# A four-layer graph network on one core: half products for the last weight, norm constants on GpSimd, and a new issue order for the main loop

## The chip, the cores and the metric

The kernel runs on one core of a Trainium2 chip. The metric is device time in microseconds (us) of one execution; the inputs are in device memory before it starts. All runs told here were fast, at a mean granted TensorE clock of 0.98 in the profiled ones, so they may be compared as they stand. Two kernels are called the same if they differ by less than 2%. A ratio is the mean time of one kernel's fast runs over that of the other's of the same rounds, so it is not quite the ratio of the medians quoted beside it; its 95% interval follows in brackets.

Engines in the profile: PE is TensorE, PEld its weight loads, DVE VectorE, ACT ScalarE, POOL GpSimd, SP SyncE. L348 is line 348 of the profiled kernel; numbers shift between kernels, because lines were added. A timeline row reads: start in us, duration in us, engine, line, operation, output<-inputs, shapes, count, and in brackets how long the engine had been idle just before and what released it.

## The reference, cut to what matters

`x` is 128 batches of 128 nodes by 256 features, in fp32. Four layers, each with a layer norm ahead and a residual behind:

```python
h = max(layernorm(x), 0);  x = x + gated_messages(h, adj)        # layer 0: three gates, two adjacency products
h = max(layernorm(x), 0);  x = x + causal_attention(h)           # layer 1: scores + adj, softmax, value, Wo
h = max(layernorm(x), 0);  x = x + A2(relu(A2(relu(A2 h W1)) W2)) W3   # layer 2: 256 -> 512 -> 1024 -> 256
h = max(layernorm(x), 0);  agg = A_hat h                         # layer 3
x = x + batchnorm(relu(batchnorm(agg W1' + b1)) W2' + b2)        # statistics over all 128*128 rows
```

(This is a condensed form of it.) Only the two batch norms of layer 3 need all batches at once. They cut the kernel into three stages: a long loop, the second product of layer 3 (512 features to 256), and the last batch norm with the residual.

## The kernel before

Batches are worked in 32 groups of four. Every layer is a Python generator that yields after each piece of work. A string, `TURN`, says from which generator the next piece is taken, and one pass through the string is one turn of the main loop. It interleaves the layers of four groups (`g - 1` to `g + 2`) and so steers the order of the instructions in every engine's queue; within a piece the queues can still mix.

```python
    TURN = "CCBCABBCDABCBBCABDDCBADCDDBDCDCBACBBCACACCCbBCBBCBCBBCBCBCBd"
    # ...
        stream = {
            "A": part(layer0, g + 2), "B": bs, "C": layer2(g), "D": ds,
            "b": part(layer1, g + 2), "d": layer3(g),
        }
        for k in TURN:
            next(stream[k], None)
```

The layer norm, four times per group. `inv_sqrt` is an add of eps on VectorE and a power of -0.5 on GpSimd:

```python
        rs = small.tile([P, G], FP, tag="rs", name=f"rs{layer}_{g}")
        inv_sqrt(rs, mv[:, :, 1], LN_EPS)
        sh = small.tile([P, G], FP, tag="sh", name=f"sh{layer}_{g}")
        nc.vector.scalar_tensor_tensor(sh, mv[:, :, 0], -1.0, rs, ALU.mult, ALU.mult)
        h = w.tile([P, G, D], FP, tag="h", name=f"h{layer}_{g}", bufs=3)
        for b in range(G):
            nc.scalar.activation(
                h[:, b, :], xt[:, b, :], AF.Relu, bias=sh[:, b : b + 1], scale=rs[:, b : b + 1]
            )
```

Most weight products of the loop are already done in seven half-size products instead of eight (Strassen's scheme in Winograd's form). That needs four sums of the activations' quarters:

```python
        engine.tensor_tensor(s1, a21, a22, ALU.add)
        engine.tensor_tensor(s2, s1, a11, ALU.subtract)
        engine.tensor_tensor(s4, a12, s2, ALU.subtract)
        engine.tensor_tensor(s3, a11, a21, ALU.subtract)
```

The second product of layer 3 is a plain one, after a per-column batch norm and ReLU on ScalarE:

```python
        for i in range(DC):
            po = bank([P, T], f"po_{g}_{i}")
            for j in range(FC):
                nc.tensor.matmul(
                    po, bw2T[:, j, i * P : (i + 1) * P], z[j],
                    start=(j == 0), stop=(j == FC - 1),
                )
            nc.vector.tensor_scalar(O[g][:, i, :], po, b2_c[:, i : i + 1], None, ALU.add)
            nc.vector.bn_stats(stats2[:, i, g, :], O[g][:, i, :])
```

## Time and profile before

The median was 2703.4 us. The stages of the profiled execution (2701.6 us):

| stage | us | limit |
|---|---|---|
| start to the first product of the second stage, with the loop's 32 turns | 2400.2 | TensorE |
| second product of layer 3 | 222.5 | TensorE |
| last batch norm, residual, output | 78.8 | transfers |

### The profile page before, as it was taken

The page shows a single profiled execution, that of the slowest core. Times are in us where ns is not written, and L with a number is a line of the kernel's source. Part 1 is how long each engine was busy: PE and PEld are TensorE (multiplying, and loading weights), DVE is VectorE, ACT ScalarE, POOL GpSimd, SP SyncE. Part 2 cuts the span into 40 slices and gives each one's busy share as a digit, 9 for nine tenths or more (in the row PEclk, how much of TensorE's full clock was granted, in tenths as well). Part 3 has the DMA queues.
Part 4 walks back from the last instruction along what each step waited for, and adds up shares of the span by engine and source line. Part 5 has one row for each costly group of instructions (what it writes and reads, how often), then busy time and mean ns, then how long its engine had stood idle before and what let it go on. Part 6 is the DMA issues. An engine that isn't in the chain of part 4 may idle for free.

```text
span 2701.6 us, 39124 instructions
## 1 busy us (share of the span) xinstructions
PE 2579.3 (95%) x14831; PEld 2216.3 (82%) x14831; DVE 1877.5 (69%) x4612; ACT 1236.5 (46%) x2447; POOL 477.2 (18%) x484
## 2 busy tenths in 40 slices
PE   3899999999999999999999999999999999979994
PEld 3788888889898898888888889889888888944443
DVE  7677777677777877777777777777777775444445
ACT  3444444444444444444444444454444443334435
POOL 3121111121111112111111111111211111110001
PEclk7999999999999999999999999999999999989998
DMA  3000000000000000000000000000000000044449
GB/s 128 8 32 17 32 32 32 32 25 31 27 30 32 32 32 32 32 32 25 24 32 32 32 32 24 32 25 32 32 32 32 32 24 24 24 148 156 156 170 367
DMA packets 61758, 142.17 MB, mean 53 GB/s; under 512 B 4594, under 2 KB 39940, under 8 KB 57604
## 3 DMA queue, kind: packets, MB, share of 16 engines
q1 hardware_dynamic: 51492, 105.21, 10.9%
q0 software_dynamic: 9216, 33.56, 3.2%
q8 instruction: 117, 1.92, 0.3%
q10 hardware_dynamic: 864, 0.92, 0.1%
q14 instruction: 69, 0.57, 0.1%
HBM read 73.08 MB, written 66.58 MB: 52 GB/s over the span
## 4 chain that ended last, share of the span: by engine, by line
PE 62%; DVE 21%; ACT 6%; issue 5%; POOL 4%; DMA 2%; ACTq 0%; DVEq 0%; POOLq 0%; SPq 0%
PE p_x L365 9%; PE po L750 8%; PE p_x L348 6%; PE pu_x L348 4%; PE p_z L365 4%; PE pz_x L365 4%; POOL rs L188 4%; DVE st L285 4%; ACT h L294 3%; DVE uT L307 3%; PE p_z L348 2%; PE pg L304 2%; PE p_y L365 2%; PE pz_z L365 2%; PE pu_z L348 2%
## 5 line engine op out<-in xcount | busy, mean ns | idle before, releaser
L294 ACT ACTIVATE h<-x,sh,rs 128x256 f32<-128x256 f32 x512 | 268.8, 592 | 144.2 <-DVE sh L291 144.2
L188 POOL TENSOR_TENSOR rs<-rs,nhalf 128x4 f32<-128x4 f32 x128 | 130.1, 1017 | 807.6 <-DVE rs L186 807.6
L365 PE MATMUL p_x<-uT,w 128*128 128x256 f32 x1024 | 242.2, 379 | 0.0
L380 ACT COPY p_t<-p_x 128x512 f32<-128x512 f32 (+1 forms) x192 | 98.3, 512 | 298.9 <-PE p_x L365 285.9
L595 ACT ACTIVATE h2T<-h2T 128x512 f32<-128x512 f32 x192 | 120.4, 627 | 232.7 <-DVE h2T L594 232.7
L750 PE MATMUL po<-zi,bw2T 128*128 128x512 f32 x496 | 213.0, 592 | 0.0
L365 PEld LDWEIGHTS p_x<-uT,w 128*128 128x128 f32 x1024 | 189.7, 190 | 23.1
L417 DVE SCALAR_TENSOR_TENSOR gs<-h,gw 128x256 f32<-128x256 f32 x384 | 198.8, 518 | 13.5 <-ACT h L294 1.3
L285 DVE BATCH_NORM_STATS2 st<-x 128x6 f32<-128x256 f32 x512 | 190.7, 414 | 3.4 <-DMA x<-in_x_dram 2.2
L750 PEld LDWEIGHTS po<-zi,bw2T 128*128 128x128 f32 x496 | 94.2, 190 | 118.6 <-issue 107.6
L743 ACT ACTIVATE zi<-zi,sh_bn,sc_bn 128x512 f32<-128x512 f32 x124 | 90.5, 802 | 117.3 <-DMA zi<-z 117.3
L625 POOL DMA_DIRECT2D x<-x x32 | 19.8, 620 | 691.5 <-DVE x L622 691.5
L754 DVE TENSOR_SCALAR o<-po,vecs 128x512 f32<-128x512 f32 x64 | 48.1, 752 | 129.1 <-PE po L750 129.1
L304 PEld LDWEIGHTS pmu<-a2T,u 128*128 128x128 f32 x1024 | 119.5, 192 | 17.1 <-issue 7.4
L348 PEld LDWEIGHTS p_x<-w,h2T 128*128 128x128 f32 x1024 | 124.3, 192 | 3.3
L365 PE MATMUL p_x<-us,w_s 128*128 128x256 f32 x512 | 126.2, 380 | 0.0
L348 PE MATMUL p_x<-w,h2T 128*128 128x128 f32 x1024 | 124.6, 275 | 0.0
L365 PE MATMUL p_x<-uT,w_s 128*128 128x256 f32 x512 | 124.3, 385 | 0.3 <-DVE h2T L594 0.3
L304 PE MATMUL pmu<-a2T,u 128*128 128x128 f32 x1024 | 119.8, 275 | 1.8 <-ACT u L561 1.8
L365 PE MATMUL p_y<-uT,w 128*128 128x256 f32 x512 | 121.1, 379 | 0.0
L365 PE MATMUL p_z<-us,w 128*128 128x256 f32 x512 | 121.0, 379 | 0.0
L365 PE MATMUL p_z<-us,w_s 128*128 128x256 f32 x512 | 121.0, 379 | 0.0
(252 smaller groups left out, 6005.0 us busy)
## 6 DMA issues: line engine op xcount, KB each, us to landing
z<-zo SPq DMA_DIRECT2D x62, 512.0 KB, 2.6
zi<-z SPq DMA_DIRECT2D x31, 1024.0 KB, 4.7
x<-in_x_dram SPq DMA_DIRECT2D x32, 512.0 KB, 3.9
x<-x POOLq DMA_DIRECT2D x32, 512.0 KB, 3.0
x3i<-x POOLq DMA_DIRECT2D x32, 512.0 KB, 6.7
out_dram<-x3i SPq DMA_DIRECT2D x64, 256.0 KB, 6.4
w<-in_L_gnn_W_dram SPq DMA_DIRECT2D x1, 2048.0 KB
w<-in_L_gnn_W_dram SPq DMA_DIRECT2D x1, 1024.0 KB
```

Source lines behind the costliest of these rows:

```text
L188: nc.gpsimd.tensor_tensor(dst, src, nhalf[:, : dst.shape[1]], ALU.pow)
L285: nc.vector.bn_stats(st[:, b, :], xt[:, b, :])
L294: nc.scalar.activation(h[:, b, :], xt[:, b, :], AF.Relu, bias=sh[:, b : b + 1], scale=rs[:, b : b + 1])
L304: nc.tensor.matmul(pm[:, b, :], src[:, b, c * P : (c + 1) * P], aT, start=True, stop=True)
L307: nc.vector.tensor_copy(dst[:, c, :], pm.rearrange("p b n -> p (b n)"))
L348: nc.tensor.matmul(pb[:, rr, :], a_r[r][:, c, rr * P : (rr + 1) * P], b_r[r][:, c, :wide], start=(first and rr == 0 and c == 0), stop=(c = ...
L365: nc.tensor.matmul(pb[:, jj, :], b_r[r][:, c, at : at + P], a_r[r][:, c, :], start=(first and jj == 0 and c == 0), stop=(c == nk - 1), ski ...
L380: nc.scalar.copy(t, pb)
L417: nc.vector.scalar_tensor_tensor(gs, h[:, b, :], 1.0, gw[:, i, :], ALU.mult, ALU.mult, accum_out=gl[:, b, i : i + 1],)
L595: nc.scalar.activation(dst, dst, AF.Relu)
L743: nc.scalar.activation(z[j], z[j], AF.Relu, bias=sh1[:, j : j + 1], scale=sc1[:, j : j + 1],)
L750: nc.tensor.matmul(po, bw2T[:, j, i * P : (i + 1) * P], z[j], start=(j == 0), stop=(j == FC - 1),)
```

## The change

It has four parts. Layer 3's second product becomes seven half products, and the next group's activations and sums are prepared while this group's products run. The layer norms' constants are worked out by GpSimd alone; in exchange its large sums go to VectorE. Two evictions of mT go to ScalarE, and one of hT's two to VectorE. `TURN` is new. The intent is to give TensorE an eighth less work in the second product, and to free VectorE from waiting for GpSimd in the loop.

```diff
-        inv_sqrt(rs, mv[:, :, 1], LN_EPS)
+        nc.gpsimd.tensor_scalar(rs, mv[:, :, 1], LN_EPS, None, ALU.add)
+        nc.gpsimd.tensor_tensor(rs, rs, nhalf[:, :G], ALU.pow)
         sh = small.tile([P, G], FP, tag="sh", name=f"sh{layer}_{g}")
-        nc.vector.scalar_tensor_tensor(sh, mv[:, :, 0], -1.0, rs, ALU.mult, ALU.mult)
+        nc.gpsimd.tensor_scalar(sh, mv[:, :, 0], -1.0, None, ALU.mult)
+        nc.gpsimd.tensor_tensor(sh, sh, rs, ALU.mult)
 # ... layer 1: hT
-            nc.scalar.copy(hT[:, c, :], pt.rearrange("p b n -> p (b n)"))
+            evict = nc.vector.tensor_copy if c else nc.scalar.copy
+            evict(hT[:, c, :], pt.rearrange("p b n -> p (b n)"))
 # ... layer 2: mT, and the sums of h2T's first half
-        mixed(mT, h, a2T, f"pm2_{g}")
+        mixed(mT, h, a2T, f"pm2_{g}", nc.scalar.copy)
-                        nc.vector if q else nc.gpsimd,
+                        nc.vector,
 # ... layer 3: the sums of gT
-        gs = sums(nc.gpsimd, quarters_t(gT), ex)
+        gs = sums(nc.vector, quarters_t(gT), ex)
 # ... the turn
-    TURN = "CCBCABBCDABCBBCABDDCBADCDDBDCDCBACBBCACACCCbBCBBCBCBBCBCBCBd"
+    TURN = "CCCBCCABBDABBCABBDDCBADCDDBDCCDBACBCCABCCACbBCBBCBCBBCBCBCdB"
 # ... second product (core)
-    EARLY = 6
+    EARLY, LATE = 4, 11
+    bw2s = keep.tile([P, 3, FC // 2, D // 2], FP, name="bw2s_late")
+    nc.scalar.dma_start(bw2s, BW2S)
+    BW2R = set_of(bw2T, bw2s)
+    def second(g):
+        # ... four activations, one yield after each
+        nc.vector.tensor_tensor(s1, a21, a22, ALU.add)
+        nc.vector.tensor_tensor(a21, a11, a21, ALU.subtract)
+        nc.vector.tensor_tensor(s2, s1, a11, ALU.subtract)
+        yield
+        def product(r, pb, first):
+            for c in range(FC // 2):
+                nc.tensor.matmul(
+                    pb, BW2R[r][:, c, :], a_r[r][:, c, :],
+                    start=(first and c == 0), stop=(c == FC // 2 - 1), skip_group_check=True,
+                )
+            if r == 1:
+                nc.vector.tensor_tensor(a12, a12, s2, ALU.subtract)
+        # ... eviction by copy or add, then the statistics
+        yield from seven(product, put, [P, T // 2], f"po_{g}", zw)
```

The diff leaves out the sums of the second weights, which GpSimd makes at the start, the way they go through device memory, and the new numbers of buffers for late blocks of x.

More of the change, by code (lines that the diff above doesn't have):

```diff
@@ L188, in inv_sqrt, with quarters, set_of, seven_of @@
         nc.gpsimd.tensor_tensor(dst, src, nhalf[:, : dst.shape[1]], ALU.pow)
+    def quarters(a):
+        k, t = a.shape[1] // 2, a.shape[2] // 2
+        return a[:, :k, :t], a[:, k:, :t], a[:, :k, t:], a[:, k:, t:]
+    def set_of(b, extra):
+        b11, b21, b12, b22 = quarters(b)
+        return b11, b21, b22, extra[:, 2], extra[:, 0], extra[:, 1], b12
+    def seven_of(b, name, extra=None):
+        b11, b21, b12, b22 = quarters(b)
+        if extra is None:
+            extra = weights.tile([P, 3, b.shape[1] // 2, b.shape[2] // 2], FP, name=f"{name}_s")
+        operands = set_of(b, extra)
+        t4n, t1, t2 = operands[3:6]
+        nc.gpsimd.tensor_tensor(t1, b12, b11, ALU.subtract)
+        nc.gpsimd.tensor_tensor(t2, b22, t1, ALU.subtract)
+        nc.gpsimd.tensor_tensor(t4n, b21, t2, ALU.subtract)
+        nc.gpsimd.tensor_tensor(b12, b22, b12, ALU.subtract)
+        return operands
     BW2T = scratch.tile([P, FC, D], FP, name="BW2T")
+    BW2S = scratch.tile([P, 3, FC // 2, D // 2], FP, name="BW2S")
+    bw2s = bw1[:, :3, :].rearrange("p a (b c) -> p a b c", b=FC // 2)
     def turned(dst, src, nr, name):
@@ L246, in prepare @@
         turned(bw2t, bw2, DC, "bw2T")
+        seven_of(bw2t, "bw2t", bw2s)
+        nc.sync.dma_start(BW2S, bw2s)
         nc.sync.dma_start(BW2T, bw2t)
@@ L297, in norm, with mixed @@
         return h
-    def mixed(dst, src, aT, name):
+    def mixed(dst, src, aT, name, evict):
         for c in range(src.shape[-1] // P):
@@ L306, in mixed @@
                 )
-            nc.vector.tensor_copy(dst[:, c, :], pm.rearrange("p b n -> p (b n)"))
-    def quarters(a):
-        k, t = a.shape[1] // 2, a.shape[2] // 2
-        return a[:, :k, :t], a[:, k:, :t], a[:, :k, t:], a[:, k:, t:]
-    def seven_of(b, name):
-        b11, b21, b12, b22 = quarters(b)
-        extra = weights.tile([P, 3, b.shape[1] // 2, b.shape[2] // 2], FP, name=f"{name}_s")
-        t1, t2, t4n = (extra[:, i] for i in range(3))
-        nc.gpsimd.tensor_tensor(t1, b12, b11, ALU.subtract)
-        nc.gpsimd.tensor_tensor(t2, b22, t1, ALU.subtract)
-        nc.gpsimd.tensor_tensor(t4n, b21, t2, ALU.subtract)
-        nc.gpsimd.tensor_tensor(b12, b22, b12, ALU.subtract)
-        return b11, b21, b22, t4n, t1, t2, b12
+            evict(dst[:, c, :], pm.rearrange("p b n -> p (b n)"))
     def sums(engine, a, extra, s3=None):
@@ L371, in columns_by_half, with seven @@
         return product
-    def seven(product, put, shape, name):
+    def seven(product, put, shape, name, pool=None):
         def kept(pb, i):
-            t = w.tile(shape, FP, tag="kept", name=f"{name}_t{i}", bufs=6)
+            t = (pool or w).tile(shape, FP, tag="kept", name=f"{name}_t{i}", bufs=6)
             nc.scalar.copy(t, pb)
@@ L566, in layer1 @@
         uT = w.tile([P, HC1, T], FP, tag="uT", name=f"uT_{g}", bufs=1)
-        mixed(uT, u, a2T, f"pmu_{g}")
+        mixed(uT, u, a2T, f"pmu_{g}", nc.vector.tensor_copy)
         ex = w.tile([P, 3, HC1 // 2, T // 2], FP, tag="us", name=f"us_{g}", bufs=1)
@@ L599, in wide @@
             )
-        s = w.tile([P, G, D], FP, tag="qv", name=f"s_{g}", bufs=1)
+        S = []
         def put_s(ij, pb, other):
             i, j = ij
-            dst = s[:, 2 * i : 2 * i + 2, j * P : (j + 1) * P]
+            if not S:
+                S.append(w.tile([P, G, D], FP, tag="qv", name=f"s_{g}", bufs=1))
+            dst = S[0][:, 2 * i : 2 * i + 2, j * P : (j + 1) * P]
             if other is None:
@@ L620, in layer2 @@
             pr = bank([P, 2, D], f"pr_{g}_{q}")
-            nc.tensor.matmul(pr, a2T, s[:, 2 * q : 2 * q + 2, :], start=True, stop=True)
+            nc.tensor.matmul(pr, a2T, S[0][:, 2 * q : 2 * q + 2, :], start=True, stop=True)
             nc.vector.tensor_tensor(
@@ L632, in layer3 @@
         gT = w.tile([P, DC, T], FP, tag="dT", name=f"gT_{g}", bufs=2)
-        mixed(gT, h, ahT, f"pg_{g}")
+        mixed(gT, h, ahT, f"pg_{g}", nc.vector.tensor_copy)
         ex = w.tile([P, 3, 1, T // 2], FP, tag="ex", name=f"gs_{g}", bufs=2)
-        gs = sums(nc.gpsimd, quarters_t(gT), ex)
+        gs = sums(nc.vector, quarters_t(gT), ex)
         yield
@@ L720 @@
     )
+    zw = zs.enter_context(tc.tile_pool(name="zw", bufs=2, side="right", reuse_waits="tile"))
     bw2T = keep.tile([P, FC, D], FP, name="bw2T")
     nc.scalar.dma_start(bw2T, BW2T)
+    bw2s = keep.tile([P, 3, FC // 2, D // 2], FP, name="bw2s_late")
+    nc.scalar.dma_start(bw2s, BW2S)
+    BW2R = set_of(bw2T, bw2s)
     ORDER = [LAST, *range(LAST)]
@@ L729, in load_z @@
         nc.sync.dma_start(z, Z[ORDER[n]])
-        ZT[ORDER[n]] = [z[:, j, :] for j in range(FC)]
+        ZT[ORDER[n]] = [z[:, :FC // 2, :], z[:, FC // 2 :, :]]
     def load_x3(g, pool, tag):
@@ L734, in load_x3, with put @@
         nc.gpsimd.dma_start(R[g], X3[g])
+    def second(g):
+        zl, zr = ZT[g]
+        ex = zw.tile([P, 2, FC // 2, T // 2], FP, tag="zs", name=f"zs_{g}")
+        a11, a21, a12, a22 = (z[:, :, i * T // 2 : (i + 1) * T // 2] for z in (zl, zr) for i in range(2))
+        s1, s2 = ex[:, 0], ex[:, 1]
+        a_r = a11, a12, a12, a22, s1, s2, a21
+        for j in range(FC):
+            z = ZT[g][j // 2][:, j % 2, :]
+            nc.scalar.activation(
+                z, z, AF.Relu, bias=sh1[:, j : j + 1], scale=sc1[:, j : j + 1],
+            )
[3 more added lines that the diff above has]
+        nc.vector.tensor_tensor(s2, s1, a11, ALU.subtract)
+        yield
+        def product(r, pb, first):
[3 more added lines that the diff above has]
+                    start=(first and c == 0), stop=(c == FC // 2 - 1), skip_group_check=True,
+                )
+            if r == 1:
+                nc.vector.tensor_tensor(a12, a12, s2, ALU.subtract)
+        done = []
+        def put(ij, pb, other):
+            i, j = ij
+            dst = O[g][:, j, i * T // 2 : (i + 1) * T // 2]
+            if other is None:
+                nc.scalar.copy(dst, pb)
+            else:
+                nc.vector.tensor_tensor(dst, pb, other, ALU.add)
+            done.append(j)
+            if done.count(j) == 2:
+                nc.vector.bn_stats(stats2[:, j, g, :], O[g][:, j, :])
+        yield from seven(product, put, [P, T // 2], f"po_{g}", zw)
     for n in range(1, 1 + AT_ONCE):
@@ L738 @@
     sc1, sh1 = bn_affine(stats1, FC, g1_c, be1_c, "bn1", b1_c)
-    ZT[LAST] = [z[:, jj, :] for z in ZT[LAST] for jj in range(2)]
+    PREPARE = FC + 1
+    now = second(LAST)
+    for _ in range(PREPARE + 1):
+        next(now)
     for n, g in enumerate(ORDER):
-        z = ZT[g]
-        for j in range(FC):
-            nc.scalar.activation(
-                z[j], z[j], AF.Relu,
-                bias=sh1[:, j : j + 1], scale=sc1[:, j : j + 1],
-            )
-        for i in range(DC):
-            po = bank([P, T], f"po_{g}_{i}")
-            for j in range(FC):
-                nc.tensor.matmul(
-                    po, bw2T[:, j, i * P : (i + 1) * P], z[j],
-                    start=(j == 0), stop=(j == FC - 1),
-                )
-            nc.vector.tensor_scalar(O[g][:, i, :], po, b2_c[:, i : i + 1], None, ALU.add)
-            nc.vector.bn_stats(stats2[:, i, g, :], O[g][:, i, :])
+        then = second(ORDER[n + 1]) if n + 1 < NG else iter(())
+        for _ in range(PREPARE):
+            next(now)
+            next(then, None)
+        next(then, None)
+        for _ in now:
+            pass
+        now = then
         if n + 1 + AT_ONCE < NG:
@@ L760 @@
     zs.close()
-    late = ctx.enter_context(tc.tile_pool(name="late", bufs=9, reuse_waits="tile"))
+    late = ctx.enter_context(tc.tile_pool(name="late", bufs=LATE, reuse_waits="tile"))
     def load_later(g):
-        load_x3(g, *((late, "x3l") if EARLY <= g < EARLY + 9 or g % 5 > 1 else (x3p, "x3")))
-    for g in range(EARLY, EARLY + 9):
+        load_x3(g, *((x3p, "x3") if g % (EARLY + LATE) < EARLY else (late, "x3l")))
+    for g in range(EARLY, EARLY + LATE):
         load_later(g)
-    sc2, sh2 = bn_affine(stats2, DC, g2_c, be2_c, "bn2")
+    sc2, sh2 = bn_affine(stats2, DC, g2_c, be2_c, "bn2", b2_c)
     for g in range(NG):
@@ L789 @@
             nc.sync.dma_start(out[at : at + 2].rearrange("b n d -> n b d"), x3[:, half, :])
-        if g + EARLY + 9 < NG:
-            load_later(g + EARLY + 9)
+        if g + EARLY + LATE < NG:
+            load_later(g + EARLY + LATE)
 _INS = [
```

## The prediction

> **What bounds the kernel now.** I read the page's slices first, then busy times by stretch, then TensorE's waits, then single instructions around the waits that repeat.
>
> The slices (each digit is tenths of 1/40 of the span) show a main loop in which TensorE is full, with a ragged head and tail:
>
> ```profile
> PE   3899999999999999999999999999999999979994
> POOL 3121111121111112111111111111211111110001
> PEclk7999999999999999999999999999999999989998
> ```
>
> Two stretches of the table of busy times (length, then busy us and instructions by engine, clock, DMA share, GB/s). The first is one turn of the main loop, which repeats every 72.21 us (between about 100 and 2339 us, 31 times); the second is the second product of layer 3 (line 750):
>
> ```profile
> 1111.68:1183.89 72.21, 71.57 (x440) 64.67 (x439) 54.82 (x138) 34.15 (x72) 13.35 (x13) 1.00 0.08 30
> 2410.00:2625.00 215.00, 212.74 (x496) 93.86 (x494) 92.82 (x128) 82.73 (x114) 3.83 (x8) 1.00 0.41 147
> ```
>
> Both are bound by TensorE at full clock. In a turn it misses only 72.21 - 71.57 = 0.64 us. TensorE's waits say which (who waited, for whom: us in all, times, longest):
>
> ```profile
> PE pu_x L348 <- DVE mT L307: 13.1, 30, 0.4
> PE pqv_y L483 <- ACT hT L474: 6.3, 30, 0.2
> ```
>
> Only these two come 30 times: 0.44 + 0.21 = 0.65 us a turn, 19.4 us in all. In order of time, one turn's first wait and the DVE work that made it late:
>
> ```profile
> 1008.92 0.16 DVE L291 SCALAR_TENSOR_TENSOR sh<-mv,rs 128x4 f32<-128x4 f32 x1 [1.13 <-POOL rs L188]
> ...
> 1012.77 0.42 DVE L609 TENSOR_TENSOR s<-p_y,p_t 128x256 f32<-128x256 f32 x1
> 1013.11 1.28 DVE L307 COPY mT<-pm 128x512 f32<-128x512 f32 x2
> ```
>
> The eviction of mT stands in VectorE's queue behind a shift that waited 1.13 us for GpSimd's power, and behind four sums. Over the run that shift costs VectorE 103.4 us of waiting in 127 times, 0.81 us each. The chain of waits carries the second product as one piece:
>
> ```profile
> 2400.24 222.52 PE po L750 x512
> ```
>
> After it, from 2622.8 to 2701.6 us, the DMA engines run at a share of 0.9 to 1.06 (314 to 401 GB/s): the last stretch, 79 us, is bound by transfers.
>
> **What the Trainium skill says.** "SBUF — State Buffer", section "Who interferes with whom": a VectorE instruction with two SBUF inputs contends with a GpSimd instruction that reads SBUF, and the second to issue blocks for the whole of the first. The trace agrees: the same gating product takes 0.42 us, and 0.82 us while GpSimd makes its sums:
>
> ```profile
> 1046.12 0.42 DVE L417 SCALAR_TENSOR_TENSOR gs<-h,gw 128x256 f32<-128x256 f32 x1
> ...
> 1047.44 0.82 DVE L417 SCALAR_TENSOR_TENSOR gs<-h,gw 128x256 f32<-128x256 f32 x1
> ```
>
> "GPSIMD Engine Reference", section "4.1 Engine selection", has GpSimd about twice as slow as VectorE for two-input elementwise work. Here a 128x512 sum takes 1.27 to 1.62 us against 0.69, a 128x256 one 0.79 to 0.89 against 0.42: it agrees. "TensorE: Matmul & The Clock Gate", section "Back-to-back issue gap", has the isolated gap grow with the columns plus a small constant. The trace: eight 128x256 records take 1.73 us (0.216 each), 128x512 ones 0.429 each, so half the columns cost half, and counting products is fair. (Each fp32 matmul shows as two records.)
>
> **The change part by part.**
>
> *Second product.* Before, a group of four batches is 8 matmuls of 512 columns, 16 records. The first 16 records took 9.6 us (restart, clock 0.73); the other 31 groups take (2622.76 - 2409.8)/31 = 6.87 us. After, seven half products of two 256-column matmuls: 28 records x 0.216 = 6.05 us. At best 0.82 us a group, 31 x 0.82 = 25 us. The other engines get more work per group. ScalarE: four activations (2.93 us in a row) and four 128x256 copies (0.37 each, some 0.31 in a row), 4.2 us. VectorE: three adds (0.42), four sums and two statistics (0.69), 5.4 us by means, about 4.7 by spacing in a row, against 2.9 before. Both fit in 6.05, but not loosely. In the built order TensorE runs products 1, 4, 5, 2, 6, then product 0 of the next group, then 3. The sharp place is a copy: ScalarE takes, after product 0 of the next group ends, a copy, an activation, a copy, two activations and the copy of product 4, about 0.31 + 0.71 + 0.31 + 1.42 + 0.37 = 3.1 us, with hand-overs 3.3. TensorE needs that bank for product 2 after four products, 3.46 us later. I allow 0.1 us a group: 31 x 0.72 = 22 us gained. The first group must have all four activations and two sums before product 4, so it gains nothing.
>
> *Norm constants.* Removed from VectorE: 128 adds (0.166) and 128 shifts (0.164), some 0.17 us per norm in a row, and 103 us of waits. Added on GpSimd: three small operations per norm. From its 128x256 and 128x512 times the fixed part is about 0.2 us, so 0.6 us beside the power's 1.02. The chain from statistics to activation is then 0.2 to 0.4 us longer, but no longer holds up the queue of VectorE.
>
> *Sums.* 512 columns x 4 and 256 columns x 4 per group leave GpSimd (166 + 100 us in all = 8.9 us a turn with contention), and add 4 x 0.6 + 4 x 0.34 = 3.8 us to VectorE. In return its gating and mixing products stop being blocked: line 417 from 518 to about 420 ns (12 a turn), lines 445, 437 and 440 from 683, 545 and 539 to 480, 350 and 350 (4 each), 3.5 us a turn.
>
> *Evictions.* Two of mT go from VectorE to ScalarE, one of hT the other way: VectorE -0.6, ScalarE +0.5 us a turn. VectorE's sum: +3.8 - 3.5 - 0.6 - 4 x 0.17 = -1 us busy and -3.2 us waiting.
>
> *Turn.* In the built order the transposes of hT now stand two long products (3.5 us) ahead of their first reader, where there was one: the 0.21 us wait should go. mT is read 1.8 us after its second matmul ends on TensorE; ScalarE makes layer 0's four activations of another group just before it. Working forward from the last product that feeds them (0.2 hand-over, 0.6 add, 1.15 residual, 1.7 statistics, 1.7 GpSimd, 2.1 activations, 0.5 copy), mT is there 0.6 to 0.9 us before it is needed. So that wait should go too. I found no other reader with less than 0.3 us. Gain: 19.4 us at best; I take 18.
>
> *Head and tail.* Head: four more GpSimd sums for the second weights (3 us, mostly beside other work), three longer norms on the path before TensorE fills: +1.5 us. Between loop and second product: one norm longer, sums faster, +0.5. Tail: only four blocks of x are loaded early where seven were; but four more can start some 9 us before the product ends and two some 6 us before, and by the first output the same fifteen are asked for. +0.5, and 0.3 for three small operations in the last constants.
>
> Sum: -22 - 18 + 1.5 + 0.5 + 0.8 = -37 us; 2703.4 - 37 = 2666 us.
>
> **The rivals.** (a) The second product stalls. VectorE or ScalarE is late for a bank in each group, as the 3.3 against 3.46 us suggests: with 0.5 us a group the gain is 10 us, the time 2678. For it: both engines at 70 to 80%, in-order queues, one bank written four times. Against: product 0 of the next group stands as a cushion, and each hand-over has most of a product's time. (b) The loop finds a new wait. The small GpSimd operations cost 0.5 us rather than 0.2, mT comes late behind ScalarE's activations: 0.4 us a turn, 12 us, time 2678. For it: the longer chain; against: GpSimd has nothing else to do. (c) All goes well and nothing is lost at the ends: -25 - 19.4 = 2659. (d) The gain at the second product is eaten by the transfers after it: if blocks of x come late, two more blocks of 0.52 MB at 390 GB/s are 2.7 us; the tail is bound by bytes already, so more than 4 us isn't likely.
>
> **Range and chances.** 2% is 54 us, below 2649.3. Even (c) doesn't reach it, as both gains are capped by idle and work that I can count: 44.7 us. Faster by over 2% would need a shorter head or tail, for which I see no cause: 0.05. Slower by over 2% needs 1.7 us a turn lost on an engine that gets fewer waits: 0.01. (a) and (b) together give the upper end, 2681; (c) with a little luck the lower, 2656.
>
> **What would show it.** TensorE's two waits of 30 times gone, a turn of 71.6 us; no wait of VectorE for GpSimd; the gating product near 420 ns throughout; GpSimd's small operations near 0.2 us; the second product in 32 groups of some 6.15 us, 200 us in all; the last stretch 79 to 80 us. It is wrong if a turn stays above 72 us, if TensorE's gap before product 2, 6 or 3 is over 0.3 us a group, or if head or tail move by more than 3 us.

## More of the kernel before

The prediction shows the slices, the waits and one turn of it. Three rows of TensorE's timeline around that turn's wait for mT are worth adding. The idle time that a row shows is not all that a wait costs:

```profile
1011.45 1.95 PE L348 MATMUL p_z<-w_s,h2s 128*128 128x128 f32 x16
1013.84 1.13 PE L348 MATMUL pu_x<-w,mT 128*128 128x256 f32 x4 [0.44 <-DVE mT L307]
1014.81 1.03 PE L348 MATMUL pu_y<-w,mT 128*128 128x256 f32 x4
```

From start to start, p_z took 2.39 us and pu_x 0.97. Unhindered groups of the same shapes take 1.79 and 0.87 (shown further down). So this wait cost 0.60 + 0.10 = 0.70 us where the bracket says 0.44.

## The result

| | before | after |
|---|---|---|
| median, us | 2703.38 | 2666.15 |
| range | 2702.99 to 2704.2 | 2663.1 to 2667.44 |
| ratio | | 0.986 [0.9843, 0.9877] |
| profiled span, us | 2701.6 | 2665.5 |
| start to first second product | 2400.2 | 2380.5 |
| second product | 222.5 | 204.2 |
| last stage | 78.8 | 80.8 |

By the 2% rule it is the same, and the total is what was predicted. The stages give -19.7, -18.3 and +2.0 us. (The end of the second product is the modelled end of its last record, in both kernels.)

The slices of the changed kernel's page (tenths of busy time in 1/40 of the span) look as before, except that GpSimd is emptier in the middle:

```profile
PE   3899999999999999999999999999999999979984
POOL 4111111111011110111111111111101111000011
PEclk7899999999999999999999999999999999989998
```

One turn, from one group's product pmu to the next, and 187 us of the second product. The columns are length, then busy us (instructions) of PE, PEld, DVE, ACT and POOL, then clock, DMA share and GB/s:

```profile
1017.97:1089.62 71.65, 71.03 (x439) 64.68 (x438) 52.30 (x137) 34.91 (x71) 8.46 (x17) 1.00 0.08 30
2390.00:2577.00 187.00, 186.11 (x837) 154.54 (x836) 147.43 (x269) 119.90 (x236) 1.07 (x2) 1.00 0.46 158
```

The turn is 71.65 us against 72.21: 16 us over the 29 turns of regular length. TensorE still misses 0.62 us of it. The list of its waits says why. Of the two waits of 30 times, hT's is gone and mT's is not; it is even longer, and its releaser is ScalarE now:

```profile
PE pu_x L360 <- ACT mT L335: 17.9, 29, 0.6
```

The gating product is quick throughout, as GpSimd makes no large sums any more (before, its mean was 518 ns). The columns after the count are busy us, mean ns, idle us before it:

```profile
L429 DVE SCALAR_TENSOR_TENSOR gs<-h,gw 128x256 f32<-128x256 f32 x384 | 163.3, 425 | 34.8 <-ACT h L322 28.8
```

Where does the wait for mT come from? Here is GpSimd in the turn of that wait, first a norm that nothing disturbs and then layer 1's norm:

```profile
991.59 0.23 POOL L315 TENSOR_SCALAR rs<-mv 128x4 f32<-128x4 f32 x1 [33.98 <-ACT h2T L608]
991.90 0.23 POOL L318 TENSOR_SCALAR sh<-mv 128x4 f32<-128x4 f32 x1
992.10 1.03 POOL L316 TENSOR_TENSOR rs<-rs,nhalf 128x4 f32<-128x4 f32 x1
993.21 0.20 POOL L319 TENSOR_TENSOR sh<-sh,rs 128x4 f32<-128x4 f32 x1
997.34 0.23 POOL L315 TENSOR_SCALAR rs<-mv 128x4 f32<-128x4 f32 x1 [3.93 <-DVE mv L313]
997.65 0.78 POOL L318 TENSOR_SCALAR sh<-mv 128x4 f32<-128x4 f32 x1
998.40 1.56 POOL L316 TENSOR_TENSOR rs<-rs,nhalf 128x4 f32<-128x4 f32 x1
1000.04 0.29 POOL L319 TENSOR_TENSOR sh<-sh,rs 128x4 f32<-128x4 f32 x1
```

The same four operations take 1.8 us from first start to last end, then 3.0. (From the start of the second to the start of the third it is 0.75 us instead of 0.20, so the delay does not rest on reported durations alone.) What VectorE does meanwhile:

```profile
997.65 0.69 DVE L343 TENSOR_TENSOR h2s<-h2T 128x512 f32<-128x512 f32 x1 [0.47 <-ACT h2T L600]
998.38 0.69 DVE L344 TENSOR_TENSOR h2s<-h2s,h2T 128x512 f32<-128x512 f32 x1
998.99 0.68 DVE L346 TENSOR_TENSOR h2T<-h2T 128x512 f32<-128x512 f32 x1
999.59 0.68 DVE L345 TENSOR_TENSOR h2s<-h2T,h2s 128x512 f32<-128x512 f32 x1
```

These are sums with two inputs in SBUF, and each of GpSimd's slow operations begins with or beside one. It is the collision that the prediction quoted from "SBUF — State Buffer", section "Who interferes with whom", the other way round: here VectorE holds what GpSimd waits for. The page says that the order of issue decides who blocks, and the trace agrees: GpSimd's 0.23 us operation takes 0.78 when it starts in the same hundredth of a microsecond as the 0.69 us sum, and 0.23 when it starts just ahead of it (run 6 below). In ScalarE's queue the copy of mT stands behind the four activations that wait for these constants, so what GpSimd delays, delays the copy:

```profile
1000.36 2.08 ACT L322 ACTIVATE h<-x,sh,rs 128x256 f32<-128x256 f32 x4 [2.74 <-POOL sh L319]
1002.35 1.04 ACT L335 COPY mT<-pm 128x512 f32<-128x512 f32 x2
```

And TensorE, with the wait at its end:

```profile
1000.39 1.95 PE L360 MATMUL p_z<-w_s,h2s 128*128 128x128 f32 x16
1002.96 1.13 PE L360 MATMUL pu_x<-w,mT 128*128 128x256 f32 x4 [0.61 <-ACT mT L335]
1003.93 1.03 PE L360 MATMUL pu_y<-w,mT 128*128 128x256 f32 x4
```

In the second product a group takes 6.27 us (product 0 of group 1 at 2388.76, of group 31 at 2576.8, over 30), not the 6.05 of 28 records in a row. TensorE shows almost no idle time there. But the bank that product 2 writes, po_z, comes free a little late. ScalarE copies it; its first activation of the next group waits for its load, 1.87 to 2.08 us in several groups, and pushes the copy of that bank back. In the chain of waits from 2376 us on, where before TensorE's products were one piece, loads of z now carry 13.0% of the time. First TensorE, then ScalarE:

```profile
2442.97 1.13 PE L775 MATMUL po_z<-zi,bw2T 128*128 128x256 f32 x4
2443.93 1.89 PE L775 MATMUL po_x<-zi,bw2T 128*128 128x256 f32 x8
```

```profile
2439.20 0.81 ACT L764 ACTIVATE zi<-zi,sh_bn,sc_bn 128x512 f32<-128x512 f32 x1 [1.87 <-DMA zi<-z]
...
2441.14 1.52 ACT L764 ACTIVATE zi<-zi,sh_bn,sc_bn 128x512 f32<-128x512 f32 x2
2442.56 0.35 ACT L392 COPY po_t<-po_z 128x256 f32<-128x256 f32 x1
```

The first of the two products after the copy takes 0.96 us from start to start instead of 0.87, and smaller losses follow: 0.2 us a group in all. That the wait for the load is behind all of it is argued, not shown: ScalarE waits some 2 us in 28 groups, yet their lengths go from 6.1 to 6.5 us, and run 11, which took away half of these waits, won back a third of the loss.

### The profile page after: what moved, and what is told of

It is laid out like the page before. It is cut to its first block, busy times and chain, and to the rows that moved or that the text cites. A ratio compares the mean times of both kernels' runs of the same rounds, so it can differ in the third digit from the quotient of the medians.

```text
span 2665.5 us, 40593 instructions
## 1 busy us (share of the span) xinstructions
PE 2541.2 (95%) x15215; PEld 2283.0 (86%) x15215; DVE 1904.5 (71%) x4743; ACT 1298.8 (49%) x2607; POOL 317.0 (12%) x616
## 4 chain that ended last, share of the span: by engine, by line
PE 81%; DVE 6%; ACT 4%; DMA 4%; POOL 3%; issue 1%; ACTq 0%; POOLq 0%; DVEq 0%; SPq 0%
PE p_x L377 15%; PE p_z L377 8%; PE p_x L360 7%; PE pu_x L360 4%; PE pmu L332 4%; PE pz_x L377 4%; PE p_y L377 4%; PE po_x L775 3%; PE p_z L360 2%; ACT h L322 2%; PE pg L332 2%; PE pm L469 2%; PE py L551 2%; PE pqv_x L501 2%; PE pqv_x L496 2%; PE ps L521 2%
## 5 line engine op out<-in xcount | busy, mean ns | idle before, releaser
L315 POOL TENSOR_SCALAR rs<-mv 128x4 f32<-128x4 f32 x128 | 29.7, 232 | 1386.9 <-ACT h2T L608 1025.7
L429 DVE SCALAR_TENSOR_TENSOR gs<-h,gw 128x256 f32<-128x256 f32 x384 | 163.3, 425 | 34.8 <-ACT h L322 28.8
L316 POOL TENSOR_TENSOR rs<-rs,nhalf 128x4 f32<-128x4 f32 x128 | 147.7, 1154 | 0.0
L574 ACT ACTIVATE u<-u 128x512 f32<-128x512 f32 x96 | 60.4, 631 | 131.8 <-DVE u L573 131.8
L764 ACT ACTIVATE zi<-zi,sh_bn,sc_bn 128x512 f32<-128x512 f32 x124 | 97.4, 812 | 55.4 <-DMA zi<-z 35.5
L377 PEld LDWEIGHTS p_z<-us,w 128*128 128x128 f32 x512 | 97.2, 190 | 13.5 <-ACT p_t L392 0.3
L377 PEld LDWEIGHTS p_z<-us,w_s 128*128 128x128 f32 x512 | 97.3, 190 | 13.2
```

Of the source, the lines that this page charges most:

```text
L316: nc.gpsimd.tensor_tensor(rs, rs, nhalf[:, :G], ALU.pow)
L377: nc.tensor.matmul(pb[:, jj, :], b_r[r][:, c, at : at + P], a_r[r][:, c, :], start=(first and jj == 0 and c == 0), stop=(c == nk - 1), ski ...
L429: nc.vector.scalar_tensor_tensor(gs, h[:, b, :], 1.0, gw[:, i, :], ALU.mult, ALU.mult, accum_out=gl[:, b, i : i + 1],)
L574: nc.scalar.activation(dst, dst, AF.Relu)
L764: nc.scalar.activation(z, z, AF.Relu, bias=sh1[:, j : j + 1], scale=sc1[:, j : j + 1],)
```

## The experiments

My theory after the traces: the wait for mT is all that separates the changed loop from its best, it comes from layer 1's blocked constants by way of ScalarE's queue, and the parts of the change add. The main rivals: the constants on GpSimd delay other things too; the large sums on VectorE are themselves the trouble; the new order does no work of its own. All twelve runs gave correct results with three rounds each. The kernel before had medians of 2703.68, 2703.55 and 2704.11 us in the three sets of runs, so runs of different sets may be compared to within about 1 us. Against it, runs 1, 2, 3 and 5 are faster by the 2% rule, 6, 11 and 12 unclear, and the others the same.

**1. mT evicted by VectorE again.** The edit to the changed kernel:

```diff
-        mixed(mT, h, a2T, f"pm2_{g}", nc.scalar.copy)
+        mixed(mT, h, a2T, f"pm2_{g}", nc.vector.tensor_copy)
```

> The changed kernel with the eviction of mT put back on VectorE. Theory: the one wait of TensorE that still comes in every turn (pu_x for ScalarE's copy of mT, 0.61 us idle) comes from the chain statistics, GpSimd constants, four activations, copy; VectorE is idle at that moment (2.8 us), so its copy is in time and the wait goes. A wait costs more than the idle shown: the gap between starts is 2.57 us where 1.78 is normal, and the first product after it takes 0.97 instead of 0.865, 0.89 us in all. Expected: a turn of 70.8 us instead of 71.65, 25 us less, 2641 us. Rival 1: only the idle shown counts: 18 us less, 2648 us. Rival 2: VectorE is late again, as it was in the kernel before: 2660 us or more.

Measured: 2639.04 us, ratio to before 0.9763 [0.9748, 0.9778]. The wait is gone from the list, and the turn is 70.77 us. The same rows of TensorE as above:

```profile
989.78 1.95 PE L360 MATMUL p_z<-w_s,h2s 128*128 128x128 f32 x16
991.57 1.03 PE L360 MATMUL pu_x<-w,mT 128*128 128x256 f32 x4
992.44 1.03 PE L360 MATMUL pu_y<-w,mT 128*128 128x256 f32 x4
```

Starts are 1.79 and 0.87 us apart, against 2.57 and 0.97 in the changed kernel: 0.78 + 0.10 = 0.88 us, which is the whole difference of the turns (71.65 - 70.77). The bracket said 0.61. The rest is 0.17 us by which p_z's modelled end overlaps the next start when nothing waits, and 0.10 us more for the first group after a stop.

**2. The two small operations ahead of the power on VectorE, in all norms.**

```diff
-        nc.gpsimd.tensor_scalar(rs, mv[:, :, 1], LN_EPS, None, ALU.add)
+        nc.vector.tensor_scalar(rs, mv[:, :, 1], LN_EPS, None, ALU.add)
...
-        nc.gpsimd.tensor_scalar(sh, mv[:, :, 0], -1.0, None, ALU.mult)
+        nc.vector.tensor_scalar(sh, mv[:, :, 0], -1.0, None, ALU.mult)
```

> The changed kernel, mT still on ScalarE, but of the four GpSimd operations of each norm the two that need no result of GpSimd (variance plus epsilon, minus mean) are on VectorE. Theory: GpSimd's chain is late because VectorE's sums of h2s, which read two operands from SBUF, block its small operations (0.78 instead of 0.23 us, 1.56 instead of 1.03). With two fewer operations the power starts before the sums and the constants come 1.2 to 1.5 us earlier; the wait for mT goes: 2641 to 2644 us. Rival: nothing is blocked, the chain is only longer by two operations of 0.23 us: the wait shrinks from 0.61 to 0.2 us idle, 2652 us.

Measured: 2639.68 us, 0.9766 [0.9749, 0.9782], turn 70.77. Here the copy of mT stayed on ScalarE and only GpSimd's chain got shorter: the power now starts before VectorE's first sum and takes 1.01 us. So it is the chain, not the engine of the copy, that matters, and either remedy takes all of the loss.

**3. The same remedy in layer 1's norm alone**, chosen by `layer == 1`.

> The changed kernel, but in the norm of layer 1 alone the first two small operations (variance plus eps, minus the mean) are on VectorE again; the other three norms stay on GpSimd alone. Theory (only layer 1's constants collide with VectorE's sums of h2T, and only they make mT late): the wait for mT goes, the turn is 70.8 us, the time 2640 us (2638 to 2644), as when all four norms were done this way (2639.7). Rival (the collisions of several norms add up): 2650 to 2660 us.

Measured: 2639.97 us, 0.9762 [0.9747, 0.9776]. **4. And in the other three norms alone** (`layer != 1`):

> The complement: the first two small operations on VectorE in every norm but layer 1's. Theory: layer 1's chain stays blocked, the turn stays at 71.6 us, the time 2665 us (2661 to 2668). Second possibility, from the run that lost less because GpSimd started 0.07 us sooner: if the schedule shifts by less than 0.1 us, [...]the time is 2650. Rival (other norms matter): under 2645 us.

Measured: 2664.51 us, 0.9853 [0.9838, 0.9867], with the wait in the list as in the changed kernel:

```profile
PE pu_x L361 <- ACT mT L336: 17.8, 29, 0.6
```

Together the two runs place the loss: one norm of four, one collision a turn.

**5. The norm constants as before** (eps and shift on VectorE, power on GpSimd), all else as changed.

> The changed kernel with the norm constants as before (epsilon and shift on VectorE, only the power on GpSimd). Theory: what is late is the chain from statistics to constants, and four GpSimd operations make it longer (3.0 us where VectorE's sums run beside it); with the old way it takes 1.4 us, so the wait for mT goes although VectorE waits for GpSimd again: 2640 to 2648 us, faster than the change. Rival: the waits of VectorE for the power (0.8 us each) come back at a place where they count, as in the kernel before: 2660 us or more.

Measured: 2642.27 us, 0.9774 [0.9757, 0.979], turn 70.81. VectorE waits for GpSimd again, 74.9 us in 98 times, and this costs TensorE next to nothing (0.04 us a turn against run 1). The wait that the change set out to remove was not a cost in this order of the loop, and removing it in the way chosen cost 24 us (2666.15 - 2642.27).

**6. The large sums back on GpSimd.**

```diff
-                        nc.vector,
+                        nc.vector if q else nc.gpsimd,
...
-        gs = sums(nc.vector, quarters_t(gT), ex)
+        gs = sums(nc.gpsimd, quarters_t(gT), ex)
```

> The changed kernel with the sums of h2s (first half) and gs back on GpSimd. Theory: those sums were never what TensorE waited for, and VectorE's slower gating products (518 instead of 425 ns) fall in stretches where nothing waits for VectorE: the time stays within 3 us of 2666, with the same wait for mT of 0.6 us. Rival: freeing VectorE of the blocked operations is what made the new turn possible: turns of 72 us or more, 2680 us.

Measured: 2650.15 us, 0.9803 [0.9788, 0.9818]. Both expectations missed: it is 16 us faster than the change, with a turn of 71.05. Layer 1's norm on GpSimd, in the same place of the turn:

```profile
992.73 0.23 POOL L315 TENSOR_SCALAR rs<-mv 128x4 f32<-128x4 f32 x1 [3.93 <-DVE mv L313]
993.04 0.23 POOL L318 TENSOR_SCALAR sh<-mv 128x4 f32<-128x4 f32 x1
993.23 1.47 POOL L316 TENSOR_TENSOR rs<-rs,nhalf 128x4 f32<-128x4 f32 x1
```

VectorE at that moment:

```profile
993.11 0.69 DVE L343 TENSOR_TENSOR h2s<-h2T 128x512 f32<-128x512 f32 x1 [0.47 <-ACT h2T L600]
```

The second operation started 0.07 us ahead of VectorE's first sum, in place of together with it, and ran unblocked: the chain is 2.46 us instead of 3.0. None of its 128 instances was slow; in the changed kernel 29 of 128 were (0.77 or 0.78 us), one in nearly every turn. These VectorE sums are those of h2T's second half, which were on VectorE in every kernel here; the sums that this run moves are others. Why GpSimd started sooner after VectorE's last statistic here (0.09 us instead of 0.16) I did not find out.

**7. The second product alone** (the kernel before with layer 3's new second product).

> The kernel before with the second product by seven half products alone (with its weights' sums, buffers and loads), all else as before. By the two traces the second product is 18.6 us shorter and the last stretch 2.2 us longer: 2687 us, with turns of 72.21 us. Rival: the stretch behaves otherwise without the new loop (the constants ready later or earlier), more than 4 us away from that.

Measured: 2684.81 us, 0.9933 [0.9918, 0.9948]. **8. The loop's parts alone** (the new norms, sums, evictions and order, with the old second product):

> The changed kernel's head and loop with the second product and last stretch of before. By the two traces head, loop and passage take 19.7 us less: 2683.5 us, with turns of 71.65 us. If the two parts add, this and the run with the second product alone give -36 to -37 us together. Rival: the parts interact (the buffers of the second product shift where the loop's tiles lie), sum off by more than 4 us.

Measured: 2683.86 us, 0.9926 [0.9911, 0.9941], turn 71.65. The two give -18.9 and -19.8 us against the same 2703.68, -38.7 together; the change's -37.2 is that within some 1.5 us. They add.

**9. The changed kernel with the old order.** The old `TURN` put back, nothing else.

> The changed kernel with the old order of the turn. Theory: the wait for hT went because the new order puts 3.5 us of other products between its transposes and its reader; with the old order it comes back (0.2 us idle, 0.48 us real): 14 us more than the change, 2680 us. Rival: the wait went because the two evictions of hT run on two engines side by side; then it stays away and the time is near 2666 us.

Measured: 2714.64 us, 1.0041 [1.0026, 1.0056], slower even than the kernel before. Both expectations missed by more than 30 us. New waits stand in TensorE's list:

```profile
PE pqv_x L496 <- ACT hT L487: 36.7, 31, 1.2
PE p_x L377 <- DVE h2T L607: 21.6, 30, 1.0
```

Again GpSimd's operations are slow (0.50, 0.51 and 1.45 us for one norm), and the copy of hT stands behind the four activations that they release.

**10. The kernel before with the new order and nothing else.**

> The kernel before with the new order of the turn and nothing else. Theory (the order gives both waits their slack, mT evicted by VectorE and hT's transposes two products ahead): turn 70.8 to 71.3 us, that is 28 to 44 us less than before, time 2660 to 2676, my figure 2668. Rival (the order pays only together with sums and evictions moved, as the old order lost 48 us when put back under them): 2695 us or more.

Measured: 2661.98 us, 0.9843 [0.9827, 0.986], turn 70.88. This is the run that changes the story. One string, on the old kernel, gives more than the whole change. Neither of the two waits is left among TensorE's repeated ones, although VectorE still evicts mT and still waits for GpSimd 127 times (98.7 us). VectorE in the same place as in the prediction's view:

```profile
991.83 0.16 DVE L291 SCALAR_TENSOR_TENSOR sh<-mv,rs 128x4 f32<-128x4 f32 x1 [1.12 <-POOL rs L188]
991.91 0.68 DVE L331 TENSOR_TENSOR h2s<-h2T 128x512 f32<-128x512 f32 x1
```

The shift waited as long as before (1.12 and 1.13 us). In the kernel before, the next sum waited another 1.15 us, for the part of h2T that ScalarE makes:

```profile
1010.23 0.69 DVE L331 TENSOR_TENSOR h2s<-h2T 128x512 f32<-128x512 f32 x1 [1.15 <-ACT h2T L587]
```

That row lay in the gap of the prediction's quotation. Why that part came late stands in ScalarE's queue, first of the kernel before, then of this run:

```profile
1009.12 0.60 ACT L294 ACTIVATE h<-x,sh,rs 128x256 f32<-128x256 f32 x1 [2.20 <-DVE sh L291]
1009.63 0.57 ACT L587 ACTIVATE h2T<-p_x 128x512 f32<-128x512 f32 x1
```

```profile
990.35 0.60 ACT L587 ACTIVATE h2T<-p_x 128x512 f32<-128x512 f32 x1 [1.30 <-PE p_x L365]
992.03 2.08 ACT L294 ACTIVATE h<-x,sh,rs 128x256 f32<-128x256 f32 x4 [1.09 <-DVE sh L291]
```

Before, h2T stood behind the first of the layer norm's four activations, and this one waited 2.20 us for the same shift: so h2T began 3.58 us after the start of its product on TensorE (1006.05), and did so in each of 30 turns. In the new order it stands ahead of all four and begins 1.93 us after its product's start (988.42). So the shift made mT late twice, in VectorE's queue and through ScalarE's; the new order takes away the second way. That this one place is the whole gain at mT is argued: the string moves many pieces.

**11. Four buffers for layer 3's loads** on top of run 1, to take away ScalarE's wait in the second product (with the early and late blocks of x set to 2 and 13 to make room).

> mT on VectorE (2639 us measured) and four instead of three buffers for the loads of the second product (two fewer early blocks of x, two more late ones). Theory: a group there takes 6.27 instead of 6.05 us because ScalarE's activations wait for their load (up to 2.3 us) and then push its bank copies late; with a fourth buffer they start earlier, TensorE loses under 0.08 us a group, the stretch is 4 to 6 us shorter: 2634 us, tail 1 us longer included. Rival: ScalarE's order alone is the cause, the activations come as late as before: within 2 us of 2639.

Measured: 2646.24 us, 0.9789 [0.9774, 0.9803]; a miss, 7 us slower than run 1. The group did get shorter (6.21 us against 6.28), with 13 waits of some 2 us on ScalarE in place of 28, but all four loads were now issued from 2346.90 us on, together with the weights (2348.07); in run 1 the last of the three had landed at 2342.28, before the weights were asked for (2345.27). Why they were issued so late I did not find out. TensorE's first product waits for the weights 10.7 us, in place of 8.0 for ScalarE:

```profile
PE po_x L775 <- DMA bw2T<-BW2T: 10.7, 1, 10.7
```

Of the two profiled executions this one began its loop 2.4 us later and the second product 5.5 us later; the second product was 1.8 us shorter, and the last stretch 3.2 us longer. The number of early blocks changed as well, so the share of each in the 7 us stays open.

**12. The last batch norm's constants ahead of the late loads** on top of run 1.

```diff
+    sc2, sh2 = bn_affine(stats2, DC, g2_c, be2_c, "bn2", b2_c)
     for g in range(EARLY, EARLY + LATE):
         load_later(g)
-    sc2, sh2 = bn_affine(stats2, DC, g2_c, be2_c, "bn2", b2_c)
```

> The changed kernel with mT evicted by VectorE (2639.0 when run alone) and the last batch norm's constants emitted ahead of the loads of the late blocks of x, so that its power does not queue behind five loads that GpSimd issues. Theory (that queue costs about 2 us of the tail): 2637 us (2635.5 to 2638.5). Rival (the late blocks then come late, and the tail is bound by bytes anyway): 2639 us or more.

Measured: 2646.56 us, 0.9787 [0.9773, 0.9802]; a miss, 7.5 us slower than run 1. The last 80 us from 2565 on, first of run 1 (which ends 8 us before the stretch does), then of this run:

```profile
2565.00:2645.00 80.00, 37.91 (x250) 28.07 (x248) 40.87 (x64) 42.46 (x61) 9.02 (x17) 0.79 0.91 328
```

```profile
2565.00:2645.00 80.00, 40.82 (x249) 30.77 (x248) 40.74 (x64) 42.36 (x61) 10.13 (x20) 0.76 1.01 372
```

80 us x (372 - 328) GB/s = 3.5 MB more were left to move. In GpSimd's queue four loads that run 1 issued between 2549 and 2553 us now stood behind a power that waits for the last statistic, and the five that run 1 issued from 2557.96 stood there too: nine were issued together from 2561.39. The power itself came no sooner (2560.56 and 2560.63 us).

## Why the prediction was right, and where it was wrong

The total was right to 0.2 us, and the range held, by luck at two levels. The first stage gained 3.7 us more than the forecast's 16, the second product 3.7 less than its 22. And within the loop two terms were wrong by more than 20 us and of opposite sign.

| order of the loop | other parts of the loop | second product | us |
|---|---|---|---|
| old | old | old | 2703.4 |
| new | old | old | 2662.0 |
| new | changed | old | 2683.9 |
| old | old | half products | 2684.8 |
| old | changed | half products | 2714.6 |
| new | changed | half products | 2666.2 |
| new | changed, mT on VectorE | half products | 2639.0 |

The order gains 42 us under the old parts (2704.1 of the same set to 2662.0) and 48 under the changed ones (2714.6 to 2666.2). The norms, sums and evictions together cost 22 us under the new order (2683.9 - 2662.0) and 30 under the old one (2714.6 - 2684.8). In no pair do they help.

- **"So that wait should go too" (mT): failed.** The step that failed is the chain worked forward with "1.7 GpSimd". It measured 3.0 us, because the sums of h2T run beside it. I had quoted the rule that two SBUF inputs on VectorE contend with GpSimd, and applied it only to VectorE's products. The sums in question were on VectorE before, too, but stood there behind the shift, which waits for the power, so they could not run beside it (run 10's rows: the shift at 991.83, the first sum at 991.91). Taking the shift off VectorE took that order away. Rival (b) named the right place, mT behind ScalarE's activations. Its cause was blocking, not slow operations: undisturbed they take 0.23 and 0.20 us, as I had said. Shortening layer 1's chain (runs 2 and 3) or taking mT out of ScalarE's queue (run 1) gives back 26 to 27 us, and the other three norms alone next to nothing (run 4).
- **What made mT late before: half right.** I put it on VectorE's queue alone, on the shift that waited for the power and four sums. The step left out is ScalarE's queue, where h2T waited behind an activation for the same shift, 1.65 us longer than in run 10; this came last (1.15 us more on VectorE), and the order removed it. Run 10 keeps the shift's wait on VectorE, and its turn is within 0.11 us of the best. So taking that wait away was not needed.
- **"Gain: 19.4 us at best": failed.** I took the idle time in the brackets for the cost. Reading starts, the old turn lost 0.70 us at mT, 0.48 at hT (0.37 to its first reader's start and 0.10 at the next), and 0.26 on two groups of products ahead of it that were slow without any bracket: 1.44 us, which is 72.21 - 70.77. Over 29 turns that is 42 us, not 19. "Perfetto Trace Analysis", section "Tensor Engine Instruction (MATMUL, LD_WEIGHTS)", says that the profiler estimates TensorE's end times; the trace agrees, since 16-record groups of 1.95 us start 1.79 us apart. So the range's lower argument, that even the best case could not reach 2%, was wrong too: runs 1, 2, 3 and 5 are 2.3 to 2.4% below before.
- **hT's wait: right.** It is gone, and it goes with the new order alone (run 10).
- **No wait of VectorE for GpSimd, gating product near 420 ns: right** (none, and 425). That it bought nothing is what runs 5 and 10 show.
- **Second product, -22 us: right in kind, too large.** It measured 18.3, and 18.9 as run 7. The term mis-sized is the 0.1 us a group for stalls: 6.27 us a group, against 6.05 of work, is 0.22, and 0.12 more over 31 groups makes the missing 3.7 us. The place is rival (a)'s copy of product 4, late after ScalarE's wait for a load; I had counted ScalarE's work and not its wait. Run 11 shows the wait's part in it, not that it is all.
- **Head and tail: small, and off.** Up to the first full turn's pmu (162.35 and 158.16 us) the loop gained 4.2 where I expected to lose 1.5; 3.5 of it lies between the first two groups' pmu, a shorter turn. After the last regular one, up to the second product, it lost 0.65 (I said 0.5). The tail lost 2.0 where I said 0.8: within it GpSimd's queue brought in 12.33 MB of x, against 11.01 before. At the 356 GB/s of this stretch the 1.32 MB more are 3.7 us of transfer, which is rival (d). That the bytes are all of it is argued, not shown; run 12 shows only that bytes pushed into the tail lengthen it.

One sum of the prediction is off, and nothing rests on it: GpSimd's sums came to 179 + 109 us, not 166 + 100, so 9.0 us a turn.

The loop came out right because the order's gain, twice what I thought possible, was halved by parts that I thought were the gain. The best kernel is the change with mT evicted by VectorE, 2639.0 us; runs 2 and 3 are within 1 us of it. By the parts' sum, the new order and the half products alone would be near 2662.0 - 18.9 = 2643 us, an estimate not run, so norms, sums and hT's eviction would then be worth some 4 us.

## What to carry to other kernels

Work out the cost of a wait on TensorE from the starts of its groups, against a turn in which nothing waits; in the kernel before the brackets showed less than half of it. When work moves between VectorE and GpSimd, look at what will run beside it in both directions: here 0.2 us operations on a chain that ends at TensorE started beside a two-input sum, and it cost 0.88 us a turn. A wait can also keep two engines apart: without it their work runs side by side. And try the reordering alone before crediting the parts that come with it.

## What the Trainium skill lacked or had wrong

- "SBUF — State Buffer", section "Who interferes with whom", holds in both directions here, but gives no size for tiny operations. A 128x4 operation of GpSimd goes from 0.23 to 0.78 us, and its power from 1.03 to 1.56, beside 0.69 us sums of VectorE. A start 0.07 us sooner decides whether the 128x4 operation is blocked (0 of 128 instead of 29); run 6, where it did, is 16 us shorter, with its other sums moved as well.
- "GPSIMD Engine Reference", section "4.1 Engine selection", gives a ratio with no tile size, and no floor for small tiles. The runs show 0.23 us for a 128x4 operation with a scalar, 0.20 with two tiles, and 1.01 to 1.04 for the power of as many elements; on VectorE the small ones take 0.16 to 0.17.
- "Perfetto Trace Analysis", section "Tensor Engine Instruction (MATMUL, LD_WEIGHTS)", says that end times are estimates, but not what follows: a wait shown as 0.61 us cost 0.88, one shown as 0.44 cost 0.70, and some lost time has no idle interval at all (0.26 us a turn).
- I saw no page that gives the time of GpSimd's queue for issuing one load. Here it is 0.53 us each, five in 2.65 us and nine in 4.76 us.
